# A scan stage that also forms another stage's keys and values: one batch formed ahead, and the output's scaling written in another place

## The chip, the cores and the metric

The kernel runs on one core of a Trainium2 chip. It is one launch that holds two decoder layers in five stages. The metric is the device time of one execution in microseconds, the median of several runs. A profile is one further execution, recorded by the hardware profiler, with a start and a length for nearly every instruction on each engine: TensorE (PE), its weight loads (PEld), VectorE (DVE), ScalarE (ACT), GpSimd (POOL), SyncE (SP), and the DMA queues.

## What is computed

The input is 16 batches of 128 tokens, 512 wide. The first stage is a selective state-space scan with a residual sum and a layer norm; cut to what matters here, with the names of the reference:

```python
A = -jnp.exp(A_log)                                        # 512 x 16
dt = softplus(einsum('bld,ed->ble', x, dt_proj_w) + dt_proj_b)
bc = einsum('bld,ed->ble', x, x_proj_w) + x_proj_b
Bs, Cs = bc[..., :16], bc[..., 16:]

def step(h, inputs):
    xt, dtt, Bt, Ct = inputs
    h = exp(dtt[..., None] * A) * h + (dtt * xt)[..., None] * Bt[:, None, :]
    return h, einsum('bdn,bn->bd', h, Ct)
# h = 0 at the first token of a batch; y is the sequence of second results
x = _layernorm(x + einsum('bld,md->blm', y, out_proj_w) + out_proj_b)
```

After it come a cross attention, a feed-forward network with ternary weights, a second layer's attention and cross attention, and a mixture of experts. The second layer's cross attention needs keys and values of `ctx_2048`, which depend on inputs alone (`memory_tokens @ wk.T` and `memory_tokens @ wv.T`):

```python
k = (memory_tokens @ wk.T).reshape(B, M, NH, HD)
v = (memory_tokens @ wv.T).reshape(B, M, NH, HD)
```

The kernel forms these already in its first stage, beside the scan, and stores them in DRAM. They are the "keys and values" of this text.

## The kernel before

**Tiles.** `stage_ssm` lays the 512 channels on partitions in four chunks (`KC`) and the tokens along the free axis. The 16 batches go in 8 parts of two (`BQ`), 256 tokens each. A part has 16 units, one for each of the 16 states n, so there are 128 units.

**A unit** is four steps. *decays* (L230): ACT writes the decay factors into a PSUM tile h, first zeros at the first token of each batch (L234), then four exponentials (L236). h has two buffers, so the decays of unit u + 2 wait for the scan of unit u to be done with it. *terms* (L240): SP issues a load BC that broadcasts the unit's rows of B and C to all partitions (L243, eight buffers), and POOL multiplies dtx by B into dBx (L245, four buffers). *scan* (L247): one DVE instruction runs h·state + dBx along the tokens, and the result is multiplied by C; for n mod 8 in 1, 4, 6 the scan goes to a tile hs (L254) and POOL multiplies (L255), otherwise it stays in h (L258) and DVE multiplies into hC (L259). *add* (L262): PE sums the 16 products of a part in PSUM by matmuls with the identity (py, L267, two banks, one buffer each). At n = 15 ACT copies the two banks out as y (L272). The next part's first add has to wait for these copies.

**Beside the units** run three generators; each `next` does one of their steps.
- *project* (L131), for the next part: pb (L136), its bias copy bc (L138), which goes to DRAM (L140) and comes back as BC, then pd in two halves (L160, L161) and softplus: Abs, Exp, +1 and Ln on ACT (L168 to L174) with sp_v on DVE (L172) and sp_u on POOL (L176), then dt on DVE (L178) and dtx on POOL (L179).
- *output* (L182), for the part before: the output projection po for each of the two batches (L189, L190), x add and statistics on DVE (L191 to L194), the rsqrt by Newton steps on DVE (L53 to L58), the shift s_sh (L198), and the scaling of two tiles on ACT (L200).
- *keys_values* (L203): for each batch of the context, a load cT (L207), 16 products pk (L211), copy kt (L214) and store (L215); then 4 products pv (L219), copy vt (L222) and store (L223).

pb, pd, po, pk and pv share two PSUM banks, "A" and "B", with one buffer each. The string `plan` (L290) says which generators take a step in unit n: k, o or n. In unit 0 of the whole stage none does. After unit 2, `load_kv` (L127) loads the weights of keys and values. The x tiles of a part, which the output adds, are loaded at its unit 0 (L297). The last step of keys_values comes after all units (L318), together with the last part's output.

**Order.** Each engine works its instructions in one fixed order. A scheduler sets that order when the kernel is built, from the order in the code and an estimate of when each is ready; `tc.keep_in_program_order` pins an instruction to its place in the code. [...] Large weights sit in rotating slots (`k.wslot()`): the first holds `dtw` and `outw`, the next `kvw`. The next stage's output weights wo reuse both.

## Time and profile before

| | us |
|---|---|
| runs | 3329.7, 3319.4, 3327.35 |
| median | 3327.35 |
| the profiled execution, its own time | 3324.17 |
| its span, first to last instruction | 3322.3 |
| scan stage, until PE's last po | 0 to 605.65 |
| first product of the next stage | 615.61 |
| DVE's first scan of the stage | 34.57 |
| first y copies of parts 2, 3 and 4 (they end part 1, 2, 3) | 179.57, 250.59, 322.0 |

So a part takes 71 us once the stage is running. The mean TensorE clock of the profile was 0.972 of full. The page of the profile shows busy time by engine, the span in 40 slices, the chain of waits that ended last, and the costliest groups of instructions by line. In a line of the timeline, the first number is the start, the second the busy time of the instructions taken together; then come engine, line, operation, output and inputs, shapes, count, and in brackets the idle time before with what ended it. In a windows table each engine has its busy time and, in brackets, its count.

```profile
L245 POOL TENSOR_TENSOR dBx<-dtx,BC 128x1024 f32<-128x1024 f32 x128 | 301.9, 2379 | 33.3 <-DVE h L258 26.0
L236 ACT ACTIVATE h<-dt,negA 128x254 f32<-128x254 f32 x512 | 239.8, 474 | 14.9 <-DVE dt L178 2.1
L258 DVE TENSOR_TENSOR_SCAN h<-h,dBx 128x1024 f32<-128x1024 f32 x80 | 183.2, 2294 | 57.6 <-ACT h L236 43.0
L267 PE MATMUL py<-hC,ident 128*128 128x512 f32 x320 | 166.9, 650 | 41.2 <-ACT y L272 36.2
```

These are the scan stage's largest groups on four engines: busy time, mean duration in ns, then the idle time before them and what ended most of it. PE's products of the sum, for example, stood 36.2 us behind the y copies.

### The profile page before, as it was taken

How to read it: one execution, taken by the hardware profiler on the slowest of the kernel's cores; microseconds unless marked ns; L12 is line 12 of the kernel's file. 1: busy time of each engine (PE TensorE's matmuls, PEld its weight loads, DVE VectorE, ACT ScalarE, POOL GpSimd, SP SyncE). 2: the span in 40 equal slices, each digit the busy share in tenths (PEclk: the TensorE clock that was granted, in tenths of full speed). 3: DMA queues.
4: the chain of work that ended last, by engine and by line, in shares of the span. 5: the costliest groups of instructions: out<-in, count | busy, mean ns of one | idle time of the engine just before them, and what ended most of it. 6: DMA issues, size and time to landing. Idle time of an engine off the chain costs nothing. (4 is left out here: it accounts for less than half of the span.)

```text
span 3322.3 us, 38519 instructions
## 1 busy us (share of the span) xinstructions
PE 3145.9 (95%) x12894; PEld 1811.7 (55%) x12944; DVE 1872.8 (56%) x4202; ACT 1379.3 (42%) x3299; POOL 1388.4 (42%) x1196
## 2 busy tenths in 40 slices
PE   6899998899999999999999989999999999999998
PEld 3444544455555555555566555666655566666665
DVE  5887878556556556556486669765553232233224
ACT  4655555233233233234433379865643231122221
POOL 6978887233333333332100066226624455333331
PEclk8999999999999999999999989999899999999999
DMA  7533332690000000001300010014435566555441
GB/s 235 134 81 97 85 85 69 227 310 8 7 4 4 7 4 4 7 0 76 112 1 1 29 36 1 11 58 150 149 115 185 193 222 210 167 180 175 160 160 62
DMA packets 162577, 317.29 MB, mean 96 GB/s; under 512 B 20233, under 2 KB 83209, under 8 KB 159300
## 3 DMA queue, kind: packets, MB, share of 16 engines
q1 hardware_dynamic: 124164, 216.23, 21.0%
q0 software_dynamic: 19200, 64.18, 5.6%
q10 hardware_dynamic: 19008, 34.35, 2.7%
q8 instruction: 105, 1.72, 0.2%
q14 instruction: 100, 0.82, 0.1%
HBM read 238.80 MB, written 129.04 MB: 111 GB/s over the span
## 5 line engine op out<-in xcount | busy, mean ns | idle before, releaser
L245 POOL TENSOR_TENSOR dBx<-dtx,BC 128x1024 f32<-128x1024 f32 x128 | 301.9, 2379 | 33.3 <-DVE h L258 26.0
L1562 PE MATMUL pg<-gu,xgT 128*128 128x352 f32 x784 | 299.4, 464 | 1.4 <-ACT act L1565 1.4
L1562 PE MATMUL pu<-gu,xgT 128*128 128x352 f32 x784 | 298.6, 463 | 0.1
L1566 DVE SCALAR_TENSOR_TENSOR act<-pu,row,act 128x352 f32<-128x352 f32 x98 | 57.1, 582 | 383.9 <-PE pu L1562 336.1
L1579 PE MATMUL y<-dn,aT 128*128 128x512 f32 x588 | 268.3, 592 | 0.0
L585 POOL TENSOR_TENSOR pr<-pr,sm 128x512 f32<-128x512 f32 x128 | 134.5, 1051 | 289.5 <-DVE sm L584 235.1
L236 ACT ACTIVATE h<-dt,negA 128x254 f32<-128x254 f32 x512 | 239.8, 474 | 14.9 <-DVE dt L178 2.1
L1605 POOL TENSOR_TENSOR x<-got,x 128x512 f32<-128x512 f32 x120 | 152.1, 1273 | 217.2 <-DMA got<-results,gidx 216.8
L616 PE MATMUL po<-w,aT 128*128 128x512 f32 x512 | 230.6, 593 | 0.5 <-DVE aT L610 0.5
L493 PE MATMUL pq<-w,xT 128*128 128x512 f32 x512 | 228.9, 594 | 0.0
L470 POOL TENSOR_TENSOR m<-m,m 128x512 f32<-128x512 f32 x96 | 121.4, 1265 | 245.3 <-DVE m L465 245.3
L1598 POOL DMA_INDIRECT got<-results,gidx x120 | 116.0, 966 | 253.0 <-DMA results<-yo 183.6
L578 ACT ACTIVATE pr<-sc,mx,sf 128x256 f32<-128x256 f32 x256 | 142.6, 561 | 188.1 <-DVE mx L571 175.8
L258 DVE TENSOR_TENSOR_SCAN h<-h,dBx 128x1024 f32<-128x1024 f32 x80 | 183.2, 2294 | 57.6 <-ACT h L236 43.0
L267 PE MATMUL py<-hC,ident 128*128 128x512 f32 x320 | 166.9, 650 | 41.2 <-ACT y L272 36.2
L1562 PEld LDWEIGHTS pu<-gu,xgT 128*128 128x128 f32 x784 | 150.3, 192 | 84.1 <-issue 2.4
L1562 PEld LDWEIGHTS pg<-gu,xgT 128*128 128x128 f32 x784 | 142.8, 192 | 65.8 <-issue 2.8
L1565 ACT ACTIVATE act<-pg 128x352 f32<-128x352 f32 x98 | 45.4, 464 | 299.6 <-PE pg L1562 278.6
L1579 PEld LDWEIGHTS y<-dn,aT 128*128 128x128 f32 x588 | 104.1, 190 | 100.8 <-issue 94.2
L1554 ACT COPY xgT<-ptx 128x512 f32<-128x512 f32 x98 | 57.3, 586 | 230.3 <-PE ptx L377 221.1
L1589 DVE COPY yo<-y 128x512 f32<-128x512 f32 x90 | 62.1, 690 | 156.7 <-PE y L1579 145.7
L493 PEld LDWEIGHTS pq<-w,xT 128*128 128x128 f32 x512 | 93.5, 190 | 102.0 <-issue 99.0
(363 smaller groups left out, 6830.5 us busy)
## 6 DMA issues: line engine op xcount, KB each, us to landing
bucket<-zeros SPq DMA_DIRECT2D x96, 388.0 KB, 8.2
row<-bucket SPq DMA_DIRECT2D x90, 388.0 KB, 3.5
BC<-bcd SPq DMA_DIRECT2D x128, 256.0 KB, 4.9
results<-yo ACTq DMA_DIRECT2D x90, 256.0 KB, 3.2
gu<-in_moe_guT SPq DMA_DIRECT2D x16, 1408.0 KB, 7.4
cT<-in_ctxT SPq DMA_DIRECT2D x32, 256.0 KB, 6.0
dn<-in_moe_downT SPq DMA_DIRECT2D x16, 512.0 KB, 6.8
rows<-r_row SPq DMA_DIRECT2D x16, 388.0 KB, 3.0
```

Source lines behind the costliest of these rows:

```text
L236: nc.scalar.activation(h[:, c, :, 1:], st.dt[:, c].rearrange("p (b t) -> p b t", b=BQ)[:, :, 1:], AF.Exp, scale=negA[:, c, n : n + 1])
L245: nc.gpsimd.tensor_tensor(dBx, st.dtx, BC[:, 0].unsqueeze(1).to_broadcast([P, KC, TQ]), ALU.mult)
L258: nc.vector.tensor_tensor_scan(hf, hf, df, 0.0, ALU.mult, ALU.add)
L267: nc.tensor.matmul(st.py[c], k.ident, st.hC[n][:, 2 * c : 2 * c + 2], start=n == 0, stop=n == NS - 1)
L470: nc.gpsimd.tensor_tensor(m1, m1, m2, ALU.add)
L493: nc.tensor.matmul(ps, src[:, c], w[c], start=c == 0, stop=c == KC - 1)
L578: nc.scalar.activation(pr[:, j], st.sc[g, i][:, j], AF.Exp, scale=st.sf[:, h : h + 1], bias=st.mx[g, i][:, j : j + 1], accum_out=sm[:, j : ...
L585: nc.gpsimd.tensor_tensor(pr, pr, sm.unsqueeze(2).to_broadcast([P, 2, 2 * P]), ALU.mult)
L616: nc.tensor.matmul(st.po, aT[:, j], k.wo[h // 8][:, h % 8], start=h == 0, stop=h == G * J - 1)
L1562: nc.tensor.matmul(ps, u.xT[:, c], gu[:, c, lo : lo + I], start=c == 0, stop=c == KC - 1)
L1579: self.nc.tensor.matmul(u.y, u.aT[:, c], u.w[1][:, c], start=c == 0, stop=c == 2)
L1605: nc.gpsimd.tensor_tensor(k.x[b], got, k.x[b], ALU.add)
```

## The change

- **Weights of keys and values.** `load_kv` is gone; the two loads are issued at once, behind the start-up loads and ahead of the context tile, the BC loads and the x loads.
- **One batch ahead.** Two steps of keys_values (pk and kt of batch 0) run before the first decays, and two more (pv and vt) in unit 0. All later batches are formed one batch earlier in the plan than before, and nothing is left for after the units. The banks of pk and pv are swapped.
- **The load of outw** is written behind those two steps. In the order that the scheduler gives ACT's queue it is still the third instruction.
- **Scaling.** `output` yields once more before the scaling, whose two instructions are kept in program order. The plan gets an "o" at n = 0, so the scaling comes in unit 0 of the next part. In ACT's order it stands behind the two y copies of the part before, within the decays of unit 5; before, it stood ahead of the decays of units 3 and 4. The rsqrt and the shift stay on DVE where they were.
- **The x loads** move from unit 0 to unit 8 of their part and are kept in order.

Each engine has the same number of instructions of each kind as before. Other places in the engines' orders move with it: in part 0 POOL's sp_u comes ahead of one product with C; in later parts ACT alternates between the exponentials of units 5 and 6 and of units 7 and 8; on PE, pk and pv of the last batch no longer stand between the output projections of the last two parts; the last vt copy stands ahead of the decays of unit 13 of the last part.

```diff
-        nc.scalar.dma_start(outw, a["outwT"].rearrange("(c p) e -> p c e", p=P))
...
-        def load_kv():
-            for i, n in enumerate(("wk", "wv")):
-                nc.sync.dma_start(kvw[:, i], a["x2_" + n + "T"].rearrange("(c p) e -> p c e", p=P))
+        for i, n in enumerate(("wk", "wv")):
+            nc.sync.dma_start(kvw[:, i], a["x2_" + n + "T"].rearrange("(c p) e -> p c e", p=P))
...
             nc.vector.scalar_tensor_tensor(shift, mv[:, :, 0], -1.0, rstd, ALU.mult, ALU.mult)
+            yield
             for i, x in enumerate(xs):
-                nc.scalar.activation(x, x, AF.Identity, scale=rstd[:, i : i + 1], bias=shift[:, i : i + 1])
+                tc.keep_in_program_order(
+                    nc.scalar.activation(x, x, AF.Identity, scale=rstd[:, i : i + 1], bias=shift[:, i : i + 1])
+                )
             yield
...
-                pk = bank("AB"[b % 2], [P, KC, P], "pk")
+                pk = bank("BA"[b % 2], [P, KC, P], "pk")
...
-                pv = bank("BA"[b % 2], [P, D], "pv")
+                pv = bank("AB"[b % 2], [P, D], "pv")
...
         kv, late, nxt = keys_values(), iter(()), iter(())
+        for _ in range(2):
+            next(kv)
+        nc.scalar.dma_start(outw, a["outwT"].rearrange("(c p) e -> p c e", p=P))
         decays(0)
         terms(0)
         terms(1)
 
-        plan = "k - n nn n nk nk n n nk nk no n ok ok k".split()
+        plan = "ok - n nn n nk nk n n nk nk no n ok ok k".split()
         for u, (st, n) in enumerate(units):
             p = u // NS
             if n == 0:
                 if p + 1 < NP:
                     nxt = project(states[p + 1], load_x(p + 1))
-                for i in range(BQ):
-                    nc.sync.dma_start(k.x[p * BQ + i], a["x"][p * BQ + i])
...
-            for what in plan[n].strip("-") if u else "":
+            for what in plan[n].strip("-") if u else "k" * 2:
                 next({"k": kv, "o": late, "n": nxt}[what], None)
             if n:
                 add(u - 1)
-            if u == 2:
-                load_kv()
+            if n == 8:
+                for i in range(BQ):
+                    tc.keep_in_program_order(nc.sync.dma_start(k.x[p * BQ + i], a["x"][p * BQ + i]))
             if n == 0 and p:
                 late = output(p - 1, states[p - 1].y)
         add(len(units) - 1)
+        for _ in late:
+            pass
         for _ in output(NP - 1, states[-1].y):
             pass
-        next(kv)
+        assert next(kv, None) is None
```

## The prediction

> **What bounds the kernel now.** I read the page first, then a table of windows, then the engines' instructions around one part boundary and at the end of the scan stage.

> ```profile
> span 3322.3 us, 38519 instructions
> ...
> PE 3145.9 (95%) x12894; PEld 1811.7 (55%) x12944; DVE 1872.8 (56%) x4202; ACT 1379.3 (42%) x3299; POOL 1388.4 (42%) x1196
> ```

> PE is the bound of the kernel as a whole. The change touches only the scan stage (0 to 606 us), so its windows matter more:

> ```profile
> core 0: us, PE busy (x) PEld busy (x) DVE busy (x) ACT busy (x) POOL busy (x), PEclk, DMA share, GB/s
> 20.00:40.00 20.00, 5.87 (x22) 3.34 (x20) 8.19 (x7) 8.48 (x19) 12.86 (x8) 0.71 0.81 255
> 236.00:307.00 71.00, 66.04 (x211) 33.36 (x210) 57.07 (x48) 41.27 (x97) 57.00 (x26) 0.95 0.37 88
> 577.00:606.00 29.00, 29.00 (x92) 13.75 (x91) 8.00 (x24) 3.74 (x6) 0.27 (x2) 1.00 0.29 92
> 606.00:616.00 10.00, 0.62 (x4) 0.42 (x2) 4.90 (x23) 2.10 (x3) 0.03 (x1) 0.63 0.84 275
> ```

> Here the reader is to see four things. At the start PE is busy 5.87 of 20 us. One steady part (236 to 307) takes 71 us, PE busy 66.04; its idle is the 4.96 us below. The tail (577 to 606) is all PE. The next stage's loads follow it at 606 to 616. ACT around the boundary:

> ```profile
> 243.16 1.52 ACT L200 ACTIVATE x<-x,s_sh,rs_y 128x512 f32<-128x512 f32 x2 [6.53 <-DVE s_sh L198]
> 245.36 0.17 ACT L234 COPY h<-zero 128x8 f32<-128x8 f32 x1 [0.68 <-DVE hs L254]
> ...
> 250.59 0.58 ACT L272 COPY y<-py 128x512 f32<-128x512 f32 x1 [0.40 <-ACT vt L222]
> ```

> And DVE, then PE, there:

> ```profile
> 242.96 0.16 DVE L198 SCALAR_TENSOR_TENSOR s_sh<-s_mv,rs_y 128x2 f32<-128x2 f32 x1
> 243.04 2.28 DVE L254 TENSOR_TENSOR_SCAN hs<-h,dBx 128x1024 f32<-128x1024 f32 x1
> ...
> 260.12 2.29 DVE L254 TENSOR_TENSOR_SCAN hs<-h,dBx 128x1024 f32<-128x1024 f32 x1 [1.68 <-PE py L267]
> ```

> ```profile
> 251.23 2.08 PE L267 MATMUL py<-hC,ident 128*128 128x512 f32 x2 [4.96 <-ACT y L272]
> ...
> 567.96 5.20 PE L189 MATMUL po<-w,y 128*128 128x512 f32 x8 [4.74 <-ACT vt L222]
> ...
> 577.68 3.60 PE L189 MATMUL po<-w,y 128*128 128x512 f32 x8
> ...
> 582.26 3.84 PE L211 MATMUL pk<-cT,w 128*128 128x128 f32 x32
> ...
> 589.37 3.60 PE L219 MATMUL pv<-w,cT 128*128 128x512 f32 x8
> ```

> ACT loses 6.53 us before the scaling. PE loses 4.96 us until the y copies free py. From 567.96 PE runs without a gap to 605.65, the stage's end.

> **1. The scaling leaves the place before the decays of units 3 and 4.** The scaling's line has 53.5 us of such waits in 8 places: six part boundaries and two at the end. It looks like the prize, but I cost it at **0**. ACT's next instruction, the zero copy of h at 245.36, waits for DVE's scan of 243.04, and that scan stands in DVE's order directly behind s_sh (242.96), for the same x add and Newton steps. With the scaling away, ACT waits at this copy until 245.3 instead. The y copies stay at 250.6, and PE's 4.96 us stay.

> **2. The scaling goes behind the two y copies.** Its two instructions (1.52 us; 807 ns each) now stand before the decays of unit 5, whose scan (254.82) already waits 1.59 us for ACT. ACT also alternates between the exponentials of units 5 and 6, then 7 and 8, so unit 5 is ready about 2.0 us later, 7 and 8 likewise. Behind unit 5's scan is unit 6's, which PE holds until 260.12 (idle 1.68 us): the cover is 1.68 us, so about 0.3 us gets out. POOL's next three dBx (264.80, 7.45 us) hide the delay of units 7 and 8 until it passes 0.5 us. Bounds +0.2 and +4 us per part; I take +0.4, the sum of what the two covers let through, for five parts: **+2 us**. With no PE gate (the last part, whose scan at 544.46 has no PE wait) it is the whole +2.0; see 5.

> **3. The start.** wk and wv (2 MB) enter SP's queue ahead of the first context tile and of the BC broadcasts, and the two x tiles (0.5 MB) leave for unit 8. Two rings moved 1.65 and 0.81 MB in 4 to 11 us, some 0.35 MB/us; the 4.5 MB now due first (xT, dtw, outw, wk, wv) end at 4 + 4.5 / 0.35 = 17 us, the context tile 1 us later. pk needs bank B, free at 25.2 (dt half 0), so no load is late; the first BC landed at 25.56 and is needed at 32.2. The second xT, behind all this on SP, landed at 38.60 and should land within 2 us of it, earlier by the x tiles' absence. ACT forms kt (0.58) before unit 0's third exponential, vt before unit 2's.

> [...] The row says pk takes 3.84 us and pv 3.60, warm. [...] PE's last pd ends at 24.83, and the window shows 0.71 granted. [...] PE idles only 0.4 us before pk, and the clock of the pd's just before was full (2.0 us for 8), so I take the row: 0. With sp_u moved earlier on POOL in part 0, the stall before one dt (2.36 us) goes, and units 2 to 4 come 1 to 3 us later: net **−1**, bounds −2.5 and +3 (rule included).

> **4. The kv schedule shifts by one batch** and the banks swap. Instruction counts are the same on each engine: **0** in steady parts. outw's load is written later, but its place on ACT's queue (third) does not change: 0. The x loads at unit 8 are read by an x add in the next part (in the tail at 601, some 50 us on) and took 7.0 us to land: 0; on SP they stand before a BC broadcast that has eight buffers of lead.

> **5. The tail.** Batch 15's pk and pv go. From start to start pk holds PE 3.67 us (582.26 to 585.93) and pv 3.43 (589.37 to 592.80). Hidden beside what? Nothing: PE is gapless there and DVE's last product ends at 579.5. **−7.1.** [...] The last part's +2.0 of item 2 comes against these; together −0.5. After the stage, the next stage's first product waits for a context tile behind wo's 2 MB, which waits for the last po: that chain moves along with PE, all later stages are PE's, so the gain passes.

> **Sum:** 2 − 1 − 7.1 − 0.5 = −6.6, to which the better half of the warm po adds 0.8: −7.4. The profiled execution took 3324.17 us, so **3317 us**. The three runs lie at 3319.4, 3327.35 and 3329.7: the median is 3.2 above the profiled one, so 3317 is 0.31% below it, on the very border of what can be told from no change (0.3%, 10 us).

> **The rivals.**
> **A, the y copies do come earlier.** If DVE's order or the earlier kv step moves the scan behind s_sh forward, PE's 4.96 us go at six boundaries: 30, with the sum's other 8: 3324 − 38 = 3286. (The slow clock behind the gap, two py's in 2.08 where four take 1.88, would go with it, about 2 us each; I leave that to DVE and ACT, which then run closer.) For it: ACT's longest wait is gone. Against: the same DVE chain holds the next copy.
> **B, slower.** Place: unit 5's decays behind y and scaling. Price: 2.0 for unit 5 plus 2 for the alternating pairs 7 and 8. It decides from the point where unit 6's scan no longer waits for PE (delay over 1.68 us), and dBx waits for scan 7 (over 0.5). Then 4 × 6 = 24 less 8: 3340. For: unit 5's scan, and others at 548.23, wait for ACT already. Against: PE's work of 66 of 71 us must be delayed, not only DVE's.
> **C, the tail is hidden.** If the first product of the next stage is held by its loads and not by PE's end (606 to 616, DMA share 0.84), only 0 to 2 us show: 3324. Against: the load was issued 1.0 us before PE's end, released by po.
> **D, the change doesn't do what it says**: true of outw's load, as above, worth nothing.

> **How the numbers follow.** Forecast 0.48 (its own range 3308 to 3325, half of it below the border: faster 0.25, same 0.23); A 0.14, faster; B 0.28 (slower 0.24, same 0.04), since unit 5's cover is just spent in my own sum; C 0.10, same. Faster 0.39, same 0.37, slower 0.24. The range leaves out most of A and the worst of B: 3297 to 3342.

> **What would show it.** Right: the 6.53 us before the scaling is gone, a wait of about 8 us stands at the zero copy instead, PE's idle before the first py of a part stays near 5; parts stay at 71 to 72 us; no pk or pv after the last scan, PE's end at 596 to 600. [...]

## The result, and the profile after

| us | before | changed |
|---|---|---|
| median | 3327.52 (8 runs, 3318.45 to 3336.66) | 3314.85 (8 runs, 3312.20 to 3316.59) |
| the profiled execution, its own time | 3324.17 | 3316.01 |
| its span | 3322.3 | 3314.2 |
| scan stage, until PE's last po | 605.65 | 595.49 |
| first product of the next stage | 615.61 | 605.50 |

The ratio of the runs is 0.9963, 95% interval 0.9950 to 0.9976: 8 to 17 us faster. The forecast was 3317. In the trace the scan stage gives 10.16 us, and the next stage starts 10.11 us earlier. At the end of the span 8.1 us of this are left. The other 2 us went in steps of a us or less between 1620 and 2700 us, in code that the change does not touch. Over the 14 profiles of this study the time from the last po to the end of the span lay between 2711.2 and 2720.6 us, so it spread by 9 us. From here on the stage is therefore measured at its own end.

The page's first lines of the changed kernel:

```profile
span 3314.2 us, 38583 instructions
...
PE 3149.4 (95%) x12944; PEld 1810.6 (55%) x12944; DVE 1875.3 (57%) x4202; ACT 1375.6 (42%) x3299; POOL 1390.3 (42%) x1196
```

PE's count is higher by 50 records than before. The weight loads (PEld) number 12944 in both, so the trace of before lacked these 50. The windows of the start and of one steady part:

```profile
20.00:40.00 20.00, 13.17 (x62) 8.68 (x62) 7.37 (x7) 9.14 (x18) 12.07 (x8) 1.00 0.87 256
236.00:307.00 71.00, 66.05 (x212) 33.45 (x212) 57.22 (x49) 40.87 (x97) 57.04 (x26) 0.95 0.39 97
```

At the start PE now has 13.17 us of work where it had 5.87, and the clock there was 1.00. The steady part is as it was: 66.05 us of PE against 66.04. ACT in that part (timeline):

```profile
243.91 0.17 ACT L234 COPY h<-zero 128x8 f32<-128x8 f32 x1 [8.72 <-DVE hs L254]
...
249.14 0.59 ACT L272 COPY y<-py 128x512 f32<-128x512 f32 x1 [0.40 <-ACT vt L222]
...
251.79 1.52 ACT L199 ACTIVATE x<-x,s_sh,rs_y 128x512 f32<-128x512 f32 x2
```

The wait of 6.53 us before the scaling has not gone. It stands as 8.72 us before the next zero copy, which waits for DVE's scan, and the y copy comes 23.36 us after the part's first scan, to the hundredth as before (250.59 − 227.23; now 249.14 − 225.78). PE in this part, at the start and in the tail:

```profile
26.08 3.84 PE L211 MATMUL pk<-cT,w 128*128 128x128 f32 x32 [0.45 <-DVE dt L175]
31.64 3.70 PE L219 MATMUL pv<-w,cT 128*128 128x512 f32 x8 [1.72 <-DVE dt L175]
...
249.78 2.08 PE L267 MATMUL py<-hC,ident 128*128 128x512 f32 x2 [4.95 <-ACT y L272]
...
564.61 5.40 PE L186 MATMUL po<-w,y 128*128 128x512 f32 x8 [2.64 <-ACT vt L222]
...
574.52 3.60 PE L186 MATMUL po<-w,y 128*128 128x512 f32 x8
```

pk and pv of batch 0 ran in the gap of the start, as fast as in the tail before (3.84 and 3.70 us, against 3.84 and 3.60). The wait for the y copies is still 4.95. In the tail the wait for vt has shrunk from 4.74 to 2.64, and no pk or pv follows.

Where the 10.16 us came from, by the first scan of each part and the tail's po:

| | before | changed | gain |
|---|---|---|---|
| first scan of the stage | 34.57 | 35.40 | −0.83 |
| part 0 | 61.98 | 59.47 | 2.51 |
| part 1 | 59.66 | 59.69 | −0.03 |
| parts 2 to 6 together | 357.13 | 357.04 | 0.09 |
| last part, first scan to the tail's first po | 54.62 | 53.01 | 1.61 |
| from that po to the stage's end | 37.69 | 30.88 | 6.81 |

### The profile page after: what moved, and what is told of

It reads as the page before. It is cut to its first block, busy times and chain, and to the rows that moved or that the text cites. A ratio compares the mean times of both kernels' runs of the same rounds, so it can differ in the third digit from the quotient of the medians.

```text
span 3314.2 us, 38583 instructions
## 1 busy us (share of the span) xinstructions
PE 3149.4 (95%) x12944; PEld 1810.6 (55%) x12944; DVE 1875.3 (57%) x4202; ACT 1375.6 (42%) x3299; POOL 1390.3 (42%) x1196
## 4 chain that ended last, share of the span: by engine, by line
PE 37%; DVE 7%; ACT 2%; POOL 2%; issue 2%; DMA 1%; another core or an unknown queue 0%; SPq 0%; POOLq 0%; DVEq 0%; ACTq 0%
PE y L1583 7%; PE pg L1566 6%; PE pu L1566 6%; PE po L787 4%; PE pu L773 2%; PE ps L1148 2%; PE pg L773 2%; PE ptx L381 1%; PE pt L381 1%; PE pw L1232 1%; PE pta L1576 1%; POOL bucket L1513 1%; DVE mx L1021 1%; ACT at_s L1202 1%; PE pts L381 1%
## 5 line engine op out<-in xcount | busy, mean ns | idle before, releaser
L267 PE MATMUL py<-hC,ident 128*128 128x512 f32 x320 | 165.4, 646 | 43.6 <-ACT y L272 37.7
```

The source lines that it names most:

```text
L267: nc.tensor.matmul(st.py[c], k.ident, st.hC[n][:, 2 * c : 2 * c + 2], start=n == 0, stop=n == NS - 1)
```

## The experiments

In each, "last po" is the end of PE's last output projection, and a part is measured from its first scan to the next part's. Parts are counted from 0. A run for which no ratio is given was executed once; there only its trace counts.

**Each half alone.** Only the scaling is moved:

```diff
+            yield
             for i, x in enumerate(xs):
-                nc.scalar.activation(x, x, AF.Identity, scale=rstd[:, i : i + 1], bias=shift[:, i : i + 1])
+                tc.keep_in_program_order(
+                    nc.scalar.activation(x, x, AF.Identity, scale=rstd[:, i : i + 1], bias=shift[:, i : i + 1])
+                )
...
-        plan = "k - n nn n nk nk n n nk nk no n ok ok k".split()
+        plan = "ok - n nn n nk nk n n nk nk no n ok ok k".split()
...
+        for _ in late:
+            pass
```

> The kernel before with the scaling alone moved behind the two y copies. Theory (the removed wait is free, because ACT's next copy waits for the same DVE chain): parts stay at 71.0 to 71.6 us, PE's wait for the y copies stays at 4.9 to 5.0 us, last po ends within 1.5 us of before's 605.65, ratio 0.999 to 1.001. Rival (the 53.5 us of ACT waits were worth something): last po ends 4 us or more earlier. Second rival (the later decays of units 5 to 8 cost): parts of 72 us or more, last po 4 us or more later.

Parts 2 to 6 took 71.2 to 71.5 us and PE's wait at their boundaries stayed at 4.93 to 4.96: for the steady part the theory was right. The ratio was 0.9996 (0.9986 to 1.0007), no difference. But the last po came at 601.96, 3.7 us earlier, where at most 1.5 were expected. Of these 0.6 are there at the last part's first scan and 3.1 come behind it: 1.6 up to the tail's first po, and 1.5 because this po then took 3.70 us where it had taken 5.20. The same is seen from the other side with the scaling back in its old place and all else of the change kept:

```diff
-            yield
             for i, x in enumerate(xs):
-                tc.keep_in_program_order(
-                    nc.scalar.activation(x, x, AF.Identity, scale=rstd[:, i : i + 1], bias=shift[:, i : i + 1])
-                )
+                nc.scalar.activation(x, x, AF.Identity, scale=rstd[:, i : i + 1], bias=shift[:, i : i + 1])
...
-        plan = "ok - n nn n nk nk n n nk nk no n ok ok k".split()
+        plan = "k - n nn n nk nk n n nk nk no n ok ok k".split()
```

> The changed kernel with the scaling back in its old place, ahead of the decays of units 3 and 4. Theory (all the gain comes from the start and from the tail): last po ends at 595 to 596 (10 us before 605.65), ratio 0.996 to 0.998. Rival (the scaling's move carries half or more of it): 600 or later.

Ratio 0.9964 (0.9951 to 0.9977), that of the whole change; last po 597.77, 7.9 us before the old kernel's and 2.3 us after the changed one's. It fell between the two expectations: most of the gain is here, but not all. The first po of the tail in PE's timeline, scaling alone and then keys and values alone:

```profile
565.77 3.70 PE L189 MATMUL po<-w,y 128*128 128x512 f32 x8 [2.65 <-ACT vt L225]
```

```profile
567.09 5.21 PE L186 MATMUL po<-w,y 128*128 128x512 f32 x8 [4.72 <-ACT vt L219]
```

The shorter wait for vt goes with the scaling's move. In the last part it changes the order that the scheduler gives ACT, and vt stands ahead of unit 13's decays. With keys and values alone the wait is the old one (before: 4.74), and what remains is the start and 7.0 us of products (from this po to the end 30.68, before 37.69).

**The price of the tail's products.** The kernel before, with the last batch's keys and values left out:

```diff
-            for b in range(NB):
+            for b in range(NB - 1):
...
                 nc.scalar.dma_start(k.x2_k[b], kt)
+                if b == NB - 2:
+                    nc.scalar.dma_start(k.x2_k[b + 1], kt)
```

(and the same for v).

> The kernel before without the products of the last batch's keys and values; the batch before it is stored twice instead, so the last batch's keys and values are left out. Theory (PE is gapless in the tail, so its work is the price): last po ends 6.8 to 7.3 us before 605.65, at 598.4 to 598.9, and 1 to 2 us earlier still if the copy that releases po(12) also comes earlier; part 0 unchanged (first scan of part 1 at 96.5). Rival (the tail's products only fill time that something else needs): 603 or later.

Last po 596.07, 9.6 us earlier, with part 0 unchanged at 61.98: as the theory had it, and 0.3 us beyond its upper end. Of these, 6.7 us lie behind the tail's first po. vt came earlier here too, with a wait of 2.23 before the first po, so the scaling's move is not the only thing that can bring it forward. Behind the last sum stands a wait of 1.67 us for the y copies, where pk and pv had stood.

**The start.** The gain of part 0 was put down to POOL's order. The first attempt pinned sp_u behind what had been written before it on POOL:

```diff
-            nc.gpsimd.tensor_tensor(u, u, v, ALU.subtract)
+            sub = nc.gpsimd.tensor_tensor(u, u, v, ALU.subtract)
+            if st is states[1] and h == 0:
+                tc.keep_in_program_order(sub)
```

> The changed kernel with one POOL subtraction of part 0 (sp_u of the first half) pinned behind the dBx that it followed in the kernel before. Theory (the start's 1.7 us come from this place in POOL's order, because DVE's dt waits for it with the next product behind it): the first scan of part 1 moves from 94.87 to 96.5 or later and last po from 595.49 to 597 or later. Rival (it comes from the batch formed ahead, or from PE): both stay within 0.5 us.

The pin changed the order of none of the four engines, so this run decides nothing between theory and rival: it is the changed kernel a second time. Part 0 took 59.45, but the last po came at 593.13, 2.4 us earlier than in the first profile of the same order. The second attempt put it behind the product of unit 6:

```diff
-            nc.gpsimd.tensor_tensor(u, u, v, ALU.subtract)
+            sub = nc.gpsimd.tensor_tensor(u, u, v, ALU.subtract)
+            if st is states[1] and h == 0:
+                behind(sub, states[0].by_C[6])
+                tc.keep_in_program_order(sub)
...
-                nc.gpsimd.tensor_tensor(hC, hC, Cn, ALU.mult)
+                st.by_C[n] = nc.gpsimd.tensor_tensor(hC, hC, Cn, ALU.mult)
```

(`behind` adds an order of issue between two instructions of one engine, without a wait.)

> The changed kernel with POOL's sp_u of part 0 (first half) put behind the hs product of unit 6, so behind one 2.35 us product, nearly where the kernel before has it. The earlier run with one pin left every engine's order as it was, so this is the test it was meant to be. Theory (part 0's 2.5 us come from this place): the step from first scan to first scan of part 0 goes from 59.47 back to 61.0 to 62.0 us. Rival (it comes from the batch formed ahead or from ACT's order): it stays at 59.3 to 59.8.

Part 0 took 63.49, 4 us more and even more than the 62 expected. DVE at its dt, changed kernel and then this one (timeline):

```profile
62.67 0.69 DVE L175 SCALAR_TENSOR_TENSOR dt<-pd,sp_u 128x512 f32<-128x512 f32 x1 [1.27 <-POOL sp_u L173]
```

```profile
64.13 0.69 DVE L182 SCALAR_TENSOR_TENSOR dt<-pd,sp_u 128x512 f32<-128x512 f32 x1 [3.69 <-POOL sp_u L177]
```

The wait at this dt grew by 2.42 us, about one product of 2.35 us, and unit 7's scan came 2.42 us later in its part. So the place sets this wait. That it makes the whole 4 us, or the gain of 2.5, is not shown. The run also altered ACT's order and the place of the second half's sp_u: unit 8's scan was only 1.09 us later, unit 9's then 3.52, behind a wait of 1.43 us for ACT. From the kernel before to the changed one sp_u moved ahead of a dBx as well as of a product with C, and the wait at this dt fell from 2.36 to 1.27 us, which is 1.1 of the 2.5 us. The run with unmixed decays below has sp_u early, with a wait of 1.28, and part 0 still took 62 us there, with 4.58 us of waiting for ACT at an earlier scan. ACT's order has a share too, and no run separates it.

**What holds a part.** The next runs ask why the steady part stayed at 71.2 to 71.6 us. First the scaling ahead of y: the y copies become a function of their own, written in unit 3 with the sums of units 0 to 2 behind them, so that pb is written ahead of these sums. The plan loses its "o" at n = 0 again.

```diff
...
+            if p and n == 3:
+                next(late, None)
+                copies(states[p - 1], pin=True)
+                late = output(p - 1, states[p - 1].y)
+                for m in range(n - 1):
+                    add(u - n + m)
...
-            if n:
+            if n and not (p and n < 3):
                 add(u - 1)
...
-            if n == 0 and p:
-                late = output(p - 1, states[p - 1].y)
```

> The changed kernel with the scaling directly ahead of the two y copies, behind the decays of unit 4. Theory (ACT's work between DVE's scan of unit 1 and the y copies lies on PE's path, each us of it for a us): PE's wait for the y copies grows from 4.95 to 6.0 to 6.6 us at six boundaries, last po ends 6 to 12 us later than 595.49. Rival (the y copies wait for something that the scaling does not touch): within 2 us of 595.49.

Both expectations missed: parts fell to 69.9 to 70.1 us and the last po to 589.52. Pb first, the scaling's place, or the two together had to be the reason. The same kernel with the scaling behind y:

```diff
-                next(late, None)
-                copies(states[p - 1], pin=True)
+                copies(states[p - 1])
+                next(late, None)
```

> The changed kernel with the sums of units 0 to 2 of a part written behind pb, and the scaling behind the y copies as in the change. It shares with the run that had the scaling ahead of y that PE works pb before the first py. Theory (that run gained because PE had pb to do while it waited for y, not because of the scaling's place): parts take 69.5 to 70.3 us as there (70.0), last po 588 to 591. Rival (the scaling ahead of y made the gain): parts stay at 71.2 to 71.6.

The theory missed again, and the rival's 71.2 to 71.6 fits: parts took 71.1 (the last of these 72.0), so pb first alone is not the reason. Then the y copies ahead of unit 4's decays, with no mixing of two units' decays and the scaling in unit 7:

```diff
...
+            if p and n == 2:
+                copies(states[p - 1])
+                for m in range(n - 1):
+                    add(u - n + m)
...
-            if n:
+            if n and not (p and n < 2):
                 add(u - 1)
...
+            if last:
+                behind(first, last[-1])
```

(`first` is a unit's zero copy, `last` holds the last exponential of each unit; the first y copy and unit 4's zero copy are tied in the same way.)

> The changed kernel with the two y copies ahead of the decays of unit 4 instead of behind them, the decays of a unit never mixed with those of the next, and the scaling in unit 7. Theory (the wait for the y copies is ACT's order, not DVE): PE's wait falls from 4.95 to 1.5 to 2.5 us at the boundaries of parts 1 to 7, PE's clock does not fall behind it (four py in 1.9 us instead of two in 2.08), parts take 66.5 to 69.5 us instead of 71.4, last po ends 12 to 30 us before 595.49, ratio 0.987 to 0.993. Rival (DVE, then held 1 us longer at unit 4's scan, becomes the bound): parts stay at 70.5 to 71.5 and last po within 5 us of 595.49.

PE's wait fell to 0.79, below what was expected, and a part still took 71.33. PE's idle time only moved (timeline):

```profile
252.55 1.98 PE L278 MATMUL py<-hC,ident 128*128 128x512 f32 x4 [0.79 <-ACT y L284]
...
293.84 2.93 PE L186 MATMUL po<-w,y 128*128 128x512 f32 x3 [4.61 <-ACT vt L222]
```

DVE waited 4.67 us for sp_u at a dt in between, longer than the 1.2 of the changed kernel. Parts 0 and 1 took 62.0 us each, together 4.9 more than in the changed kernel; that the last po still came at 592.55 is from the last part and the tail. The ratio was 0.9945 (0.9928 to 0.9962). The mixing alone:

> The changed kernel with the exponentials of one unit never mixed with those of the next. Theory (the mixed order and the scaling behind y cost units 5 to 8 about 1.7 us each, but PE's own work covers it): last po within 1.5 us of 595.49. Rival (the mixed order is what makes a part longer): last po 4 us or more earlier.

Its edit is the `last` lines above, on the changed kernel. Last po 594.86: as the theory had it in sum, though by luck, since parts 0 and 1 took 62 us each (2.5 more) and three later parts 70.0 to 71.2. Then dt's wait was taken away from the run with y early: sp_u before two dBx that are needed later, pb first, and the unmixed decays only in units 5 and 6.

```diff
+            if n == 10 and NS < u < (NP - 1) * NS:
+                behind(made, states[u // NS + 1].sub)
```

> The run with y early, with pb written ahead of the first py, the unmixed decays only in units 5 and 6, and POOL's sp_u of a part's first half ahead of the dBx of units 10 and 11. Theory (with y early, the part was held by DVE's dt waiting 4.67 us for sp_u, behind two dBx that nobody needs yet): dt's wait falls to 2 us or less, parts take 67 to 69.5 us, last po 572 to 588, ratio 0.986 to 0.992. Rival (another wait of the same length takes its place, so the part is held by more than one loop): parts at 70.5 to 71.5.

The wait at that dt was gone, and yet parts took 70.7 to 71.1, as the rival had it. Now PE's idle time stood in three places, before pb (1.32), pd (1.31) and po (3.10). The last po came at 587.23, the earliest of all runs and within what the theory expected, with parts 0 and 1 at 59.5 and 60.0 and a shorter tail. The ratio was 0.9952 (0.9936 to 0.9969), outside the theory's 0.986 to 0.992.

The runs with pb first left one pair to separate: PE's work behind the y copies, and the scaling in front of unit 5's decays. First the changed kernel with nothing altered but the scaling's unit:

```diff
-        plan = "ok - n nn n nk nk n n nk nk no n ok ok k".split()
+        plan = "k - n nn n nk nk n n nk nk no n ok ok k".split()
...
             if n == 0 and p:
-                late = output(p - 1, states[p - 1].y)
+                before, late = late, output(p - 1, states[p - 1].y)
+            if n == 7 and p:
+                next(before, None)
```

> The changed kernel with the scaling in unit 7 instead of unit 0 of the next part, so behind neither the y copies nor ahead of the decays of unit 5. Theory (the later decays of units 5 to 8 are covered by PE and by POOL, as the sum of the prediction had it, with 0 measured): DVE's wait at unit 5's scan falls from 3.3 to 1.6 us, yet parts stay at 71.0 to 71.6 us and last po within 2 us of the changed kernel's 593 to 595.5. Rival (the scaling's place behind y costs the part about its 1.5 us): parts of 69.5 to 70.2, last po 585 to 589.

and then this together with pb first.

> As the last, with pb written ahead of the first sums too (as in the run that took 71.1 us for a part with the scaling behind y). Theory (two loops of nearly the same length hold a part: PE from the y copies on, and DVE through unit 5's decays; each must be relieved for a gain): with both relieved parts take 69.3 to 70.2 us, last po 584 to 589, ratio 0.992 to 0.996. Rival (pb first is worth nothing and the run with the scaling ahead of y gained by accident): parts at 70.8 to 71.5.

With the scaling alone out of the way, three parts took 71.6 to 71.7 us and two 70.0 and 70.8; last po 596.64, ratio 0.9966 (0.9954 to 0.9979). The last section shows what the two shorter parts have of their own. With both, all five parts took 69.5 to 69.9, as the theory expected, last po 588.98, ratio 0.9947 (0.9930 to 0.9963). DVE's scans of units 5 and 6 tell why. The lines are from four kernels in this order: the changed kernel, the scaling in unit 7, pb first, and both.

```profile
255.06 2.30 DVE L258 TENSOR_TENSOR_SCAN h<-h,dBx 128x1024 f32<-128x1024 f32 x1 [3.27 <-ACT h L236]
...
258.59 2.28 DVE L254 TENSOR_TENSOR_SCAN hs<-h,dBx 128x1024 f32<-128x1024 f32 x1
```

```profile
253.79 2.30 DVE L258 TENSOR_TENSOR_SCAN h<-h,dBx 128x1024 f32<-128x1024 f32 x1 [1.59 <-ACT h L236]
...
259.36 2.29 DVE L254 TENSOR_TENSOR_SCAN hs<-h,dBx 128x1024 f32<-128x1024 f32 x1 [1.96 <-PE py L267]
```

```profile
255.05 2.30 DVE L258 TENSOR_TENSOR_SCAN h<-h,dBx 128x1024 f32<-128x1024 f32 x1 [3.42 <-ACT h L236]
...
258.58 2.28 DVE L254 TENSOR_TENSOR_SCAN hs<-h,dBx 128x1024 f32<-128x1024 f32 x1
```

```profile
251.81 2.30 DVE L258 TENSOR_TENSOR_SCAN h<-h,dBx 128x1024 f32<-128x1024 f32 x1 [1.59 <-ACT h L236]
...
255.34 2.28 DVE L254 TENSOR_TENSOR_SCAN hs<-h,dBx 128x1024 f32<-128x1024 f32 x1
```

Take out the scaling, and unit 5's wait falls from 3.27 to 1.59, but unit 6 then waits 1.96 for PE. Take out PE's delay, and unit 5's 3.42 still stands. Only with both out do both waits go, and unit 6's scan starts 31.1 us after the part's first scan instead of 32.8, 33.2 and 33.0 (first scans at 225.78, 226.20, 225.62 and 224.23). The part is then 1.7, 2.1 and 1.5 us shorter than in the other three. The scaling is not the whole of DVE's loop. In the run with unmixed decays it stands in front of unit 5's last exponentials too, unit 5 waits 2.99 us and unit 6 starts at 32.7, and yet one part took 69.99, where PE was late by little (last section). Unit 7 starts at 35.1 there instead of 36.6 in the changed kernel, so the alternation of units 7 and 8 belongs to the loop. Nor are these the only limits: in the two runs with y early unit 6's scan starts 30.5 to 30.9 us after the first, and a part still took 70.7 to 71.3. Taking the wait for sp_u away gave 0.6 us of that; what holds the rest, and what holds the part of 69.6, is open.

The version with both beat the kernel before by 0.53%. Against the changed kernel its median is 7 us lower (3307.87 to 3314.85), but the two intervals overlap, and the two were timed in different series, in which the kernel before differed by 2.7 us (3324.80 and 3327.52). It is better by the trace (last po 6.5 us earlier); by the runs this is likely but not shown. In its tail the wait before the first po is 3.12 us and that po takes 6.55 us, so moving the scaling there gives back some of what the change had won.

## Why the prediction was right, step by step

In the kernel before, DVE's scan of unit 5 stood here (timeline); the changed kernel's, at 255.06, is the first of the four above.

```profile
254.82 2.30 DVE L258 TENSOR_TENSOR_SCAN h<-h,dBx 128x1024 f32<-128x1024 f32 x1 [1.59 <-ACT h L236]
```

- **The wait that goes is worth nothing (item 1): right.** 6.53 became 8.72 at the next copy, with the y copies at 23.36 us after the first scan in both kernels.
- **The scaling behind y (item 2): mechanism right, term too large.** Unit 5's scan stood 27.59 us behind the part's first scan (254.82 − 227.23). In the changed kernel it is 29.28 (255.06 − 225.78): 1.69 us later, forecast 2.0. The cover of 1.68 us at unit 6 took it; the +2 for five parts measured −0.1 in sum. It was not covered everywhere: the first of these parts became 0.2 us longer. The run with the scaling in unit 7 shows the cover come back as 1.96 us. The last part, with no PE wait at unit 6, was to pay +2.0. Its unit 5 came 1.7 later, but none of this reached the tail's first po, which waits for the vt copy.
- **The start (item 3): right in sign, −1.7 against −1.** The forecast had the dt wait of 2.36 us go; it fell to 1.27, and ACT's order has a share that is not separated. The first scan came 0.83 us later, but not because of pk: PE's first pd, ahead of it, took 2.94 us instead of 2.03. That is no fixed cost of the change. In the eleven profiles with this start the first pd took 1.99 to 3.22 us and the first scan came at 34.45 to 35.92. The upper bound of +3 counts on a slower pk as well, an estimate that no run shows: pk took 3.84 us and pv 3.70, near the rows, at a granted clock of 1.00. The forecast for the second xT was wrong without harm: in the run with keys and values alone, whose start is the same, it landed at 42.64, 4 us later than before, yet no product waited for it.
- **The tail (item 5): −7.1 for pk and pv, measured 7.0 with the keys and values alone; right.** The −0.5 stands for −1.2 from the vt copy, which ends PE's 4.74 us gap and now comes ahead of unit 13's decays, −1.6 from a warm po (5.20 us to the 3.60 of the full clock), and the last part's +2.0. What was attributed wrongly and mis-sized is the vt copy's term: I took its move as part of the shift of keys and values. It belongs to the scaling's move: the gap is 2.65 with that alone and 4.72 without it. With the last part's own delay it was to give 0.5 us and gave 1.6. The warm po was to add 0.8. That it follows from a shorter gap was my estimate, and no run shows it: behind 2.64 us po cost 0.2 in the profile of the change (5.40 against 5.20 us), and behind 2.65 us it gave 1.5 in the repetition and with the scaling alone (3.70).
- **The sum:** 7.4 forecast, 10.16 at the end of the stage, 8.2 between the profiled executions, 12.7 between medians. The last po at 595.49 lies half a us ahead of the 596 to 600 that were to show it right. Some of the nearness is luck: the 7.4 were taken from the profiled execution, 3.2 us under the median; taken from the median they make 3320. The sum has a slip as well. Item 5's terms −1.2, −1.6 and +2.0 make −0.8, not −0.5, and the sum then counts half of the warm po once more; added up as they stand, all terms give 3317 with a warm po and 3318 with half of it.
- **Rivals.** A did not happen: the same DVE chain held the copies, as argued against it. B named the right place and price (2 us at unit 5) and the right point from which it decides. In most parts that point was not reached, because PE held unit 6 about as long. It is reached when pb goes first, and where PE is late by less (last section). C did not happen: the next stage's first product came 10.01 us behind PE's end, before 9.96.

## What to carry to other kernels

A long wait on an engine is worth only what the next instruction of that engine does not wait for anyway: look up the releaser of the one behind it. When two loops through different engines have nearly one length, relieving one can show nothing, even with an engine at 93% of its time; the test is to relieve both at once. In a kernel whose order a scheduler chooses, compare the order of every engine first: a move in one place can reorder a tail far away, and a pin can change nothing.

## What the hardware showed that was not expected

The TensorE clock fell in one run and not in another, with the same instructions behind the same gap. The tail's first po in the changed kernel (above) took 5.40 us behind 2.64 us of idle time; in its repetition with the same order:

```profile
563.95 3.70 PE L188 MATMUL po<-w,y 128*128 128x512 f32 x8 [2.65 <-ACT vt L224]
```

In the first, its eight products took 0.70, 0.59, 0.70, then four of 0.95 to 1.06, then 0.59: the slow stretch began 1.5 us after PE had restarted. This is 1.7 of the 2.4 us by which these two profiles differ.

```profile
562.51:565.92 3.41, 1.31 (x3) 1.00 0.95 362
565.92:569.33 3.41, 3.41 (x5) 0.50 0.22 86
```

```profile
562.31:565.72 3.41, 1.77 (x4) 1.00 0.92 353
565.72:569.13 3.41, 3.41 (x8) 1.00 0.16 61
```

In the first, 2.10 us of the gap lie in one step, and half clock follows; in the repetition 1.64 do, the rest lies in the step before, and the clock stays full.

The length of a part goes with the same records. In the parts below, the products behind the wait of 4.95 us at the part's start were slow for 2.97 to 6.36 us after PE's restart, until the half-clock stretch ended:

| kernel | half clock after the restart, us | part, us |
|---|---|---|
| before, parts 2 to 6 | 5.10, 5.76, 6.07, 6.23, 6.32 | 71.02, 71.37, 71.52, 71.59, 71.63 |
| scaling in unit 7, parts 5, 6 and 4 | 2.97, 4.61, 6.36 | 70.04, 70.83, 71.66 |
| unmixed decays, parts 4, 5 and 3 | 3.01, 4.70, 6.33 | 69.99, 70.83, 71.59 |
| changed, parts 2, 3 and 6 | 5.07, 5.53, 6.36 | 71.22, 71.22, 71.62 |
| changed, repetition, part 6 | 3.00 | 71.20 |

In the first three kernels each us of half clock went with half a us more for the part (70.04 to 71.66 us for 2.97 to 6.36). In the changed kernel the part took 71.22 us with 5.07 us of half clock and 71.20 with 3.00 in the repetition. There the other loop holds it, through the scaling and the alternating decays, as rival B had it. In the run with the scaling in unit 7 this separates the part of 70.0 us from the three of 71.6:

```profile
393.48 2.08 PE L267 MATMUL py<-hC,ident 128*128 128x512 f32 x2 [4.95 <-ACT y L272]
395.48 1.06 PE L133 MATMUL pb<-xT,xpw 128*32 128x256 f32 x2
396.48 1.12 PE L267 MATMUL py<-hC,ident 128*128 128x512 f32 x2
```

Here the second pair of py took 1.12 us; in the parts of 71.6 it took 2.08. So one profile does not price a gap like the tail's 2.65 us: the same gap was worth 0 and 1.7 us.
